# Attention and FFN kernel: row sums folded by a chain of accumulating transfers into one product

## The chip, the cores and the metric

The kernel runs on one core of a Trainium2 chip. A core has a tensor engine (PE; its weight loads are listed as PEld), a vector engine (DVE), a scalar engine (ACT), GpSimd (POOL), a sync engine (SP) that here only issues transfers, and sixteen DMA engines that all queues share. The metric is the device time of one execution in microseconds.

## The reference

The input x is (2, 2048, 512) in float32. One pre-norm transformer block is computed: layer norm, attention with 16 query heads and 2 key/value heads of 32 dimensions with rotary embedding, a residual, a second layer norm, a product with a weight that has been rounded to e4m3 (activations too), and a residual.

```python
scores = jnp.einsum('bqhd,bkhd->bhqk', q, k_exp) * hd ** (-0.5)
attn = jax.nn.softmax(scores, axis=-1)
out = jnp.einsum('bhqk,bkhd->bqhd', attn, v_exp).reshape(b, s, d)
return out @ wo + bo
...
x = x + _L0_attn_ref(_layernorm(x, axis=-1), ...)
x = x + _L0_ffn_ref(_layernorm(x, axis=-1), L0_ffn_weight)
```

What matters below is the softmax: each query's exponentials are summed over all 2048 keys, and the sum of exponentials times values is divided by that sum.

## The kernel before, in words

The tokens are cut into 8 blocks of 512, four per batch. Keys and values of the first batch are projected in a front part. Then the attention runs over 64 *units*: 8 blocks x 4 groups of four heads ("quads") x 2 halves of 256 queries. Side work (projections of the next block, the output product of the last one, second layer norms, the weight's rounding) is cut into small steps; `fill` puts one step at fixed places in the order of instructions. A last part does the FFN.

A unit has four *rounds* (r = 0 to 3), each over four chunks of 128 keys. The order is written out by hand (line 997 on). In a round PE computes:

- eight scores `s` (L517) for the *next* unit's row maxima, each into one of three PSUM banks, from which DVE takes a maximum (L524, into `part`). `more_scores(n)` emits n of them. When side work holds one of the three banks (`lent[0]` is not None), scores have two;
- four `T` (L963), the scores of this unit minus their maxima, 128 keys x (4 heads x 256 queries), alternating between two PSUM areas E and O. ACT makes `p = exp(T)` from each (L972), into four buffers in turn;
- the value products `avs` (L913) of the four p, 32 matmuls, into the first half of a PSUM bank `avs`.

The sums over keys are not made by PE from every p. POOL adds p of chunks 0 and 1 into `pair` (two buffers) and p of chunks 2 and 3 into a tile of `far_sums` (four buffers, L946 for both). Then a transfer that POOL issues adds `pair` to `far_sums[r]` in SBUF (`accum_op=add`, 512 KB, L1020). In round 2 one more such transfer adds `far_sums[0]` to `far_sums[1]` (L1022). So a unit leaves three tiles to be summed, 1 to 3 of `far_before` as the next unit calls them. That next unit multiplies them with ones on PE (`sum_up`, L927, eight matmuls for each tile) into the second half of its own `avs` bank: two tiles at the end of its round 0, the third at the end of its round 1. After that a job `finish_heads` copies the sums to `both[:, 1]` (L885), DVE takes two reciprocals (L889), and POOL multiplies values and reciprocals (L890). `both[:, 0]`, the values, is copied from `avs` at the unit's end (L1038); `both` has one buffer.

Every engine executes its queue in order. A POOL instruction that waits for a transfer holds all that POOL has behind it, and so does a PE matmul that waits for a tile.

Of the kernel before, what the change touches and what calls it, by code (L numbers as in the profile page):

```python
# [8 lines left out]
F32 = mybir.dt.float32  # L9
# [4 lines left out]
ALU = mybir.AluOpType  # L14
AX = mybir.AxisListType

P = 128
# [10 lines left out]
def preln_attn_fp8_ffn_kernel(  # L28
# [37 lines left out]
    nc = tc.nc  # L66
# [9 lines left out]
    HB = 256  # L76
# [16 lines left out]
    w2 = ctx.enter_context(tc.tile_pool(name="w2", bufs=6))  # L93
# [13 lines left out]
    lent = [S_BANKS - 1]  # L107

    def s_bank():

        if s_next[0] == lent[0]:
            s_next[0] = (s_next[0] + 1) % S_BANKS
        tag = f"s{s_next[0]}"
        s_next[0] = (s_next[0] + 1) % S_BANKS
        return tag
# [354 lines left out]
    units = [(k, half) for k in range(len(quads)) for half in range(HALVES)]  # L470
# [28 lines left out]
    def split_maxima():  # L499

        if split:
            mview, mx = split.pop()
            nc.gpsimd.tensor_tensor(
                mview[:, :, :, 1], mx, mview[:, :, :, 0].bitcast(F32), ALU.subtract
            )
# [131 lines left out]
    def fetch_y_over_keys(n, what, g):  # L637

        y_near[n] = stacked[what][:, g, :].bitcast(F32).rearrange("p (i d) -> p i d", i=NT)
        nc.sync.dma_start(y_near[n], y_far[n])  # L640
# [122 lines left out]
    def fill(kind, pieces=1):  # L763

        for _ in range(pieces):
            ready = [job for job in queue if job.due <= step[0] and not job.waits()]
            if lent[0] is not None:
                ready = [job for job in ready if job is owner[0]]
            able = [
                (jobs, job)  # L770
                for jobs, some in ((finishing, finishing[:1]), (queue, ready), (beside, beside))
                for job in some
                if job.kind in (kind, OTHER) and job.due <= step[0]
            ]
            if able:
                do(*able[0])
# [41 lines left out]
    def stack_next(u):  # L818
        k, half = units[u]
        n, quad = quads[k]  # L820

        if half == 0:
            if k + 1 < len(quads) and k + 1 not in qst:
                while quads[k + 1] not in q_raw:
                    advance()
                stack_queries(k + 1)
        b = batch(k)
        if b + 1 < B and n == (b + 1) * NB - 1 and quad == 2 and half == 1:
            while (b + 2) * NB - 1 not in keys_done:
                advance()  # L830
            fetch_keys("kS", b + 1, 0)
            fetch_keys("dkS", b + 1, 0)
        if b > 0 and n == b * NB and quad == 0 and half == 0:
            fetch_keys("kS", b, 1)
            fetch_keys("dkS", b, 1)
# [69 lines left out]
    def columns(u, chunks, probs, av):  # L905

        k, half = units[u]
        for kc, p in zip(chunks, probs):
# [3 lines left out]
            for j in range(4):  # L912
# [7 lines left out]
                    skip_group_check=True,  # L920
                )

    def sum_up(dst, parts, start, stop):

        for i, part in enumerate(parts):
            for j in range(4):
                nc.tensor.matmul(  # L927
                    dst[j * HD : (j + 1) * HD, :],
                    ones,
                    part[:, j, :],  # L930
                    start=start and i == 0,
                    stop=stop and i == len(parts) - 1,
                    tile_position=(0, j * HD),
                    skip_group_check=True,
                )

    def add_pair(u, kc, a, b):
        far = kc % ROUND == 2
        pa = papool.tile(
            [P, 4, HB],  # L940
            F32,
            tag="pa" if far else "pair",
            name=f"pa_{u}_{kc}",
            bufs=4 if far else 2,
        )
        nc.gpsimd.tensor_tensor(pa, a, b, ALU.add)  # L946
        return pa

    def probabilities(u, T, kc):

        k, half = units[u]
        if kc < 2:
            for j in range(4):
                nc.tensor.matmul(  # L954
                    T[:, j, :],
                    sel[:, j, :],
                    maxima[u],
                    start=(j % 2 == 0),
                    stop=True,
                    skip_group_check=True,  # L960
                )
        for j in range(0, 4, 2):
            nc.tensor.matmul(  # L963
                T[:, j : j + 2, :],
                stacked["dkS"][:, group(k), kc * P : (kc + 1) * P],
                qst[k][:, j : j + 2, half * HB : (half + 1) * HB],
                start=False,
                stop=True,
                skip_group_check=True,
            )  # L970
        p = ppool.tile([P, 4, HB], F32, tag="p", name=f"p_{u}_{kc}")
        nc.scalar.activation(p, T, AF.Exp, scale=SCALE)  # L972
        return p

    def more_scores(n):
        for _ in range(n):
            next(scores, None)

    with tc.manual_schedule():
        more_scores(LEAD)  # L980
        for u, (k, half) in enumerate(units):
            n, quad = quads[k]
            if half == 0 and quad == 0:
                attn_of[n] = wide.tile(
                    [P, QUADS, TB], F32, tag="attn", name=f"attn_{n}", bufs=2
                )
            stack_next(u)
            banks = [
                ps_t.tile([P, 4, HB], F32, tag="EO"[parity], name=f"T_{u}_{parity}")
                for parity in range(2)  # L990
            ]

            far_sums = []
            whole = u == len(units) - 1
            ending_soon = u >= len(units) - 2
            pieces = 2 if ending_soon else 1
            for r in range(ROUNDS):
                chunks = list(range(r * ROUND, (r + 1) * ROUND))
                step[0] += 1
                while r == 1 and landing:  # L1000
                    landing.pop()()
                if r == 2:
                    ask(u)
                last = r == ROUNDS - 1
                more_scores(2 if r == 0 else 1)
                probs = [probabilities(u, banks[0], chunks[0])]
                more_scores(0 if r == 0 else 1)
                probs.append(probabilities(u, banks[1], chunks[1]))
                pair = add_pair(u, chunks[0], *probs)
                more_scores(2)  # L1010
                if r > 0:
                    fill(ON_PE, pieces)
                probs.append(probabilities(u, banks[0], chunks[2]))
                more_scores(2)
                probs.append(probabilities(u, banks[1], chunks[3]))
                if ending_soon:
                    fill(ON_DVE)
                if not (last and whole):
                    far_sums.append(add_pair(u, chunks[2], *probs[2:]))
                    nc.gpsimd.dma_start(out=far_sums[r], in_=pair, accum_op=ALU.add)  # L1020
                if r == 2:
                    nc.gpsimd.dma_start(out=far_sums[1], in_=far_sums[0], accum_op=ALU.add)  # L1022
                fill(ON_PE, pieces)
                more_scores(2)
                split_maxima()
                fill(ON_DVE, 3 if finishing else 2)
                if r == 0:
                    avs = ps_av.tile([P, 2, HB], F32, tag="av", name=f"avs_{u}")
                columns(u, chunks, probs, avs[:, 0, :])


                if u > 0 and r == 0:
                    sum_up(avs[:, 1, :], far_before[1:3], False, False)
                elif u > 0 and r == 1:
                    sum_up(avs[:, 1, :], far_before[3:], False, True)
                    finishing.append(Job(finish_heads(u - 1, both, avs[:, 1, :])))
            both = w2.tile([P, 2, HB], F32, tag="both", name=f"both_{u}", bufs=1)
            nc.scalar.copy(both[:, 0, :], avs[:, 0, :])  # L1038
            far_before = far_sums
        sums = ps_s.tile([P, TB], F32, tag=s_bank(), name="sums_last")[:, :HB]  # L1040
        sum_up(sums, [pair, *probs[2:], *far_sums[1:]], True, True)
        finishing.append(Job(finish_heads(u, both, sums)))
        fetch_y_over_keys(2, "kS", 1)
        attending[0] = False
        for jobs in (finishing, queue, beside):
            while jobs:
                jobs[0].step()
                if jobs[0].kind is None:
                    jobs.pop(0)
# [122 lines left out]
```

## Time and profile before

| | |
|---|---|
| median of 3 runs | 2327.25 us (2326.39 to 2331.35) |
| profiled execution | 2329.9 us |
| span of its instructions | 2327.9 us |
| mean granted PE clock | 0.975 |
| PE busy | 2141.7 us (92%) |
| DVE busy | 1706.0 us (73%) |
| POOL busy | 1766.2 us (76%) |
| ACT busy | 1237.9 us (53%) |
| transfers by POOL's queue (q0) | 175.66 MB, 40.1% of sixteen engines' span |

A line of the profile names the source line, the engine, the operation, the tiles written and read, and how often. "[0.72 <-ACT p L972]" is the engine's idle time ahead of it and what ended it. In a table of windows, each engine has its busy time in that stretch and, in brackets, the number of its instructions; the last three columns are the granted PE clock as a share of full speed, the share of the sixteen DMA engines' time that was busy, and GB/s. The attention takes up about 126 to 2215 us of the span; the 64 units in it take 27.3 to 43.6 us each.

### The profile page before, as it was taken

The numbers are of one execution on the slowest core, as the hardware profiler recorded it, in microseconds if no ns is written. First come the engines' busy times: TensorE is split into PE (matmuls) and PEld (weight loads), VectorE is DVE, ScalarE is ACT, GpSimd is POOL, SyncE is SP. The second block draws the span as 40 slices with busy tenths as digits, with TensorE's granted clock in tenths as the row PEclk, the third lists the DMA queues.
The fourth block names the chain that finished last, engine by engine and source line by source line (L and its number), as shares of the span: only waits on it lengthen the run. The fifth ranks groups of instructions, "written<-read, shape, count | busy, mean of one in ns | idle before, by whom it ended". The sixth has DMA issues, their size and how long they took to land. (4 is left out here: it accounts for less than half of the span.)

```text
span 2327.9 us, 39404 instructions
## 1 busy us (share of the span) xinstructions
PE 2141.7 (92%) x15506; PEld 1239.0 (53%) x15506; DVE 1706.0 (73%) x2679; ACT 1237.9 (53%) x1545; POOL 1766.2 (76%) x1199
## 2 busy tenths in 40 slices
PE   5499999999999999999999999999999899899945
PEld 3255555555555555555555555555555555555522
DVE  3467778776777776876777778676977977767578
ACT  2146556655556555655555555554655555545546
POOL 3268889988877987889878878887888777877810
PEclk9699999999999999999999999999999999999978
DMA  6646656666466765658486556664665645847512
GB/s 197 169 102 137 136 114 163 143 141 131 94 163 135 158 129 135 145 121 194 99 206 141 108 124 147 133 118 95 135 149 120 141 99 126 171 89 196 109 55 109
DMA packets 116410, 312.76 MB, mean 134 GB/s; under 512 B 16896, under 2 KB 17536, under 8 KB 112384
## 3 DMA queue, kind: packets, MB, share of 16 engines
q0 software_dynamic: 50160, 175.66, 40.1%
q1 hardware_dynamic: 63648, 133.21, 19.4%
q8 instruction: 121, 1.98, 0.3%
q10 hardware_dynamic: 2416, 1.38, 0.2%
q14 instruction: 65, 0.53, 0.1%
HBM read 91.56 MB, written 42.99 MB: 58 GB/s over the span
## 5 line engine op out<-in xcount | busy, mean ns | idle before, releaser
L524 DVE TENSOR_REDUCE part<-s 128x1 f32<-128x512 f32 x2048 | 1312.8, 684 | 525.4 <-PE s L517 523.5
L946 POOL TENSOR_TENSOR pa<-p,p 128x1024 f32<-128x1024 f32 x511 | 1241.4, 2479 | 283.6 <-ACT p L972 261.2
L972 ACT ACTIVATE p<-T 128x1024 f32<-128x1024 f32 x1024 | 1002.5, 1024 | 583.0 <-PE T L963 554.6
L517 PE MATMUL s<-kS,qst 128*128 128x512 f32 x2048 | 865.9, 465 | 89.2 <-DVE part L524 27.2
L963 PE MATMUL T<-qst,dkS 128*128 128x512 f32 x2048 | 698.2, 423 | 3.1 <-ACT p L972 2.0
L517 PEld LDWEIGHTS s<-kS,qst 128*128 128x128 f32 x2048 | 383.3, 190 | 491.8 <-DVE part L524 277.8
L913 PE MATMUL avs<-p,vX 128*32 128x256 f32 x8192 | 509.5, 383 | 1.1 <-ACT p L972 1.1
L963 PEld LDWEIGHTS T<-qst,dkS 128*128 128x128 f32 x2048 | 366.3, 189 | 138.7 <-issue 52.0
L913 PEld LDWEIGHTS avs<-p,vX 128*32 128x32 f32 x8192 | 233.6, 110 | 214.3 <-issue 79.6
L1020 POOL DMA_DIRECT2D pa<-pa x255 | 224.2, 879 | 80.4 <-POOL pa L946 75.6
L301 PE MATMUL po<-wo_sb,attn 128*128 128x512 f32 x256 | 130.2, 594 | 1.3 <-POOL attn L890 1.3
L889 DVE RECIPROCAL both<-both 128x128 f32<-128x128 f32 x128 | 112.4, 919 | 11.2 <-ACT both L885 11.2
L301 PE MATMUL pq<-xnT_q,wq_sb 128*128 128x512 f32 x224 | 114.3, 592 | 0.0
L927 PE MATMUL avs<-pa,ones 128*32 128x256 f32 x1512 | 105.5, 382 | 6.8 <-DMA pa<-pa 6.8
L885 ACT COPY both<-avs 128x256 f32<-128x256 f32 x63 | 23.4, 372 | 133.2 <-PE avs L927 133.2
L890 POOL TENSOR_TENSOR attn<-both 128x256 f32<-128x256 f32 x64 | 84.8, 1326 | 5.9 <-DVE both L889 5.9
L954 PEld LDWEIGHTS T<-mT,sel 128*128 128x128 f32 x512 | 78.4, 189 | 13.0 <-ACT mT L546 1.5
L954 PE MATMUL T<-mT,sel 128*128 128x256 f32 x512 | 81.7, 282 | 0.6 <-ACT mT L546 0.6
L1022 POOL DMA_DIRECT2D pa<-pa x64 | 74.2, 1159 | 5.4 <-DMA pa<-pa 5.0
L927 PEld LDWEIGHTS avs<-pa,ones 128*32 128x32 f32 x1512 | 49.3, 111 | 39.8 <-DMA pa<-pa 7.3
L546 ACT CAST mT<-mtp 128x256 fp32r<-128x256 f32 x64 | 23.8, 371 | 84.1 <-PE mtp L542 84.1
L532 ACT CAST mrow<-mx 128x8 fp32r<-128x8 f32 x64 | 13.1, 205 | 93.6 <-DVE mx L531 93.6
(126 smaller groups left out, 1157.5 us busy)
## 6 DMA issues: line engine op xcount, KB each, us to landing
pa<-pa POOLq DMA_DIRECT2D x319, 512.0 KB, 4.9
qst<-q_far SPq DMA_DIRECT2D x128, 256.0 KB, 4.6
x_kv<-in_L_attn_x_dram SPq DMA_DIRECT2D x8, 1024.0 KB, 8.7
q_far<-hi_q SPq DMA_DIRECT2D x32, 256.0 KB, 4.4
q_far<-lo_q SPq DMA_DIRECT2D x32, 256.0 KB, 3.7
x_res<-in_L_attn_x_dram SPq DMA_DIRECT2D x8, 1024.0 KB, 8.8
x_res<-in_L_attn_bo_dram POOLq DMA_DIRECT2D x8, 1024.0 KB, 11.8
out_dram<-v SPq DMA_DIRECT2D x16, 512.0 KB, 2.8
```

Of the source, the lines that this page charges most:

```text
L301: nc.tensor.matmul(dst, lhs(c), rhs(c), start=(c == 0), stop=(c == chunks - 1))
L517: nc.tensor.matmul(s, qst[k][:, j, at : at + P], stacked["kS"][:, group(k), kb * TB : (kb + 1) * TB], start=True, stop=True,)
L524: nc.vector.tensor_reduce(part[:, i, j, kb : kb + 1], s, AX.X, ALU.max)
L889: nc.vector.reciprocal(piece, piece)
L890: nc.gpsimd.tensor_tensor(attn_of[n][:, quad, half * HB : (half + 1) * HB], both[:, 0, :], both[:, 1, :], ALU.mult)
L913: nc.tensor.matmul(av[j * HD : (j + 1) * HD, :], vX[batch(k)][:, kc, group(k), :], p[:, j, :], start=(kc == 0), stop=(kc == NTS - 1), tile ...
L927: nc.tensor.matmul(dst[j * HD : (j + 1) * HD, :], ones, part[:, j, :], start=start and i == 0, stop=stop and i == len(parts) - 1, tile_pos ...
L946: nc.gpsimd.tensor_tensor(pa, a, b, ALU.add)
L954: nc.tensor.matmul(T[:, j, :], sel[:, j, :], maxima[u], start=(j % 2 == 0), stop=True, skip_group_check=True,)
L963: nc.tensor.matmul(T[:, j : j + 2, :], stacked["dkS"][:, group(k), kc * P : (kc + 1) * P], qst[k][:, j : j + 2, half * HB : (half + 1) * H ...
L972: nc.scalar.activation(p, T, AF.Exp, scale=SCALE)
L1020: nc.gpsimd.dma_start(out=far_sums[r], in_=pair, accum_op=ALU.add)
```

## The change

For every unit but the last three (`in_one`), two more accumulating transfers are issued in the next unit: tile 1 is added to tile 2 after the first addition of round 0, and tile 2 to tile 3 after the first addition of round 1. Tile 3 then holds the whole unit's sums, and one `sum_up` of eight matmuls follows at the end of round 2 in place of those at the ends of rounds 0 and 1. The finishing starts a round later. `both` gets a second buffer. And where a bank is lent at the start of rounds 1 to 3, both scores ahead of the second probability are now emitted ahead of the first one, as round 0 always does.

```diff
+    def in_one(u):
+
+        return 0 <= u < len(units) - 3
+
...
                 last = r == ROUNDS - 1
-                more_scores(2 if r == 0 else 1)
+
+                before = 1 if r > 0 and lent[0] is None else 2
+                more_scores(before)
                 probs = [probabilities(u, banks[0], chunks[0])]
-                more_scores(0 if r == 0 else 1)
+                more_scores(2 - before)
                 probs.append(probabilities(u, banks[1], chunks[1]))
                 pair = add_pair(u, chunks[0], *probs)
+
+                if r < 2 and in_one(u - 1):
+                    at = r + 2
+                    nc.gpsimd.dma_start(
+                        out=far_before[at], in_=far_before[at - 1], accum_op=ALU.add
+                    )
                 more_scores(2)
...
-                if u > 0 and r == 0:
+                if u > 0 and r == 0 and not in_one(u - 1):
                     sum_up(avs[:, 1, :], far_before[1:3], False, False)
-                elif u > 0 and r == 1:
+                elif u > 0 and r == (2 if in_one(u - 1) else 1):
                     sum_up(avs[:, 1, :], far_before[3:], False, True)
                     finishing.append(Job(finish_heads(u - 1, both, avs[:, 1, :])))
-            both = w2.tile([P, 2, HB], F32, tag="both", name=f"both_{u}", bufs=1)
+            both = w2.tile([P, 2, HB], F32, tag="both", name=f"both_{u}", bufs=2)
             nc.scalar.copy(both[:, 0, :], avs[:, 0, :])
             far_before = far_sums
```

## The prediction

> **What bounds the kernel now.** I read the page first, then the waits, then the timeline of TensorE (PE) and of GpSimd (POOL) for single units, then windows cut at the first score-of-probability matmul (T<-qst,dkS) of each round.
>
> ```profile
> PE 2141.7 (92%) x15506; PEld 1239.0 (53%) x15506; DVE 1706.0 (73%) x2679; ACT 1237.9 (53%) x1545; POOL 1766.2 (76%) x1199
> ...
> q0 software_dynamic: 50160, 175.66, 40.1%
> ...
> L927 PE MATMUL avs<-pa,ones 128*32 128x256 f32 x1512 | 105.5, 382 | 6.8 <-DMA pa<-pa 6.8
> ```
>
> PE looks like the bound, and the products with ones (L927) hold 105.5 us of it. But three engines stand above 70%, so what a product is worth has to be read inside a round. The PE timeline of one unit, the ends of its rounds 0, 1 and 2:
>
> ```profile
> 1007.14 1.93 PE L913 MATMUL avs<-p,vX 128*32 128x256 f32 x32
> 1008.89 1.05 PE L927 MATMUL avs<-pa,ones 128*32 128x256 f32 x16
> 1009.87 0.50 PE L517 MATMUL s<-kS,qst 128*128 128x512 f32 x1
> ...
> 1015.71 1.93 PE L913 MATMUL avs<-p,vX 128*32 128x256 f32 x32
> 1017.46 0.61 PE L927 MATMUL avs<-pa,ones 128*32 128x256 f32 x8
> 1018.01 0.50 PE L517 MATMUL s<-kS,qst 128*128 128x512 f32 x1
> ...
> 1022.34 1.94 PE L913 MATMUL avs<-p,vX 128*32 128x256 f32 x32
> 1024.20 0.50 PE L517 MATMUL s<-kS,qst 128*128 128x512 f32 x1
> ```
>
> From the first value product to the next score it takes 2.73, 2.30 and 1.86 us: each eight sum matmuls cost 0.43 to 0.44 us, on PE's own path, since the score follows without a wait. POOL in an idle unit (so I call one without side work on PE; the others are full ones):
>
> ```profile
> 1678.78 4.73 POOL L946 TENSOR_TENSOR pa<-p,p 128x1024 f32<-128x1024 f32 x2 [0.72 <-ACT p L972]
> 1683.81 0.87 POOL L1020 DMA_DIRECT2D pa<-pa  x1 [0.30 <-POOL pa L946]
> 1684.39 1.18 POOL L1022 DMA_DIRECT2D pa<-pa  x1
> ```
>
> Two additions, a transfer's issue, and idle time of 0.72 us: POOL is close behind PE. A second issue directly after the first moves POOL's end from 1684.68 to 1685.57: 0.89 us each. Windows over whole units (span, PE, PEld, DVE, ACT, POOL, clock, DMA share, GB/s):
>
> ```profile
> 1032.40:1066.80 34.40, 33.77 (x243) 19.47 (x242) 23.18 (x38) 18.62 (x24) 33.13 (x22) 1.00 0.81 190
> 1600.30:1634.20 33.90, 33.17 (x240) 19.16 (x239) 24.48 (x40) 17.40 (x21) 24.22 (x16) 1.00 0.44 89
> ```
>
> In the first POOL's 33.13 us plus four waits of 0.30 us leave nothing; in the second 8.5 us are free. And the DMA engines in rounds 1 and 2 of a unit that begins a block, with the landing of the two pair transfers issued there:
>
> ```profile
> 1440.30:1446.90 6.60, 6.57 (x58) 3.98 (x57) 5.08 (x8) 4.08 (x5) 6.14 (x4) 1.00 0.77 188
> 1446.90:1453.10 6.20, 6.17 (x50) 3.76 (x49) 5.97 (x10) 4.23 (x6) 2.19 (x3) 1.00 1.04 300
> ```
>
> ```profile
> DMA to landing us min/median/max: 9.0/9.8/10.5
> ```
>
> There the engines are full; over the whole kernel the median landing is 4.7 us. POOL is busy for only 2.19 of 6.2 us there: it waits for a landing already.
>
> **The change, part by part.** The profiled execution took 2329.9 us (span 2327.9), 2.65 above the median of the runs, 2327.25; I sum against 2329.9 and take the difference to the median.
>
> *Sum matmuls.* For 61 units (u-1 from 0 to 60) 24 become 8: 16 fewer, 2 x 0.435 = 0.87 us, 61 x 0.87 = 53.1 us. The vector engine (DVE) would hide some if it were busy when the score is ready; before the first reduction of rounds 1 and 2 it sits idle 0.35 to 2.1 us in the units I read, so I count nothing back. The page's busy time would say 105.5 x 16/24 x 61/63 = 68; it holds the tails of matmuls that overlap.
>
> *POOL's two added issues.* 122 issues between the two additions of rounds 0 and 1, 0.89 us each: 1.8 us a unit. Taking each unit's POOL busy time plus 4 x 0.30 from its length, 49 of 61 units have over 2.67 us idle (0.87 + 1.8) and lose nothing. Twelve don't: those starting at 188.6, 354.1, 410.7, 767.6 and 1032.4 have about none (shortfall 2.59 to 2.66 each, 13.1 together), those at 501.8 and 1993.1 have 1.07 (1.6 each), five more fall short by 0.14 to 0.93 (2.4). Together 18.7 us given back. Inside an idle unit, rounds 0 and 1 need 2 x 2.35 + 0.89 + 1.16 = 6.75 us of POOL in a PE round of 6.2, and the buffer of p for the third chunk was free only 1.8 us ahead: about 0.45 us late in ten such units, 5 us (0 to 12).
>
> *The transfers' landing.* 122 more of 512 KB; q0 moves 175.66 MB in 40.1% of 2328 us, so one takes 2.79 us of all sixteen engines, 340 in all: the DMA share goes from 0.62 to about 0.78. The product of round 2 now waits for a chain of two. Behind it on PE's queue stands everything: scores, probabilities, value products. In a quiet unit the second link is issued after the first addition of round 1, lands 4.7 us later, and is needed 6.7 us or more after its issue: hidden. Where q0 is backed up I put its landing at the later of issue + 4.7 and the round-0 pair's landing + 2.8, against the end of round 2's value products less 1.31 us. Thirteen units come out late: those starting at 382.8, 1171.1, 1433.0, 1690.6 and 1965.2 by 5.0, 5.6, 6.0, 5.2 and 4.1 us, eight others by 0.2 to 2.4, 38.7 in all. Off this come 5.1 in three units that POOL holds anyhow, 2.5 that two of them wait already, and about 3 at 2029, where PE now waits 6.84 us for such a landing (POOL's buffers will hold it there still, but later). I take 28, with ends of 5 (a landing of 4.5, the shortest, hides most) and 60 (17.4, the longest that a chained transfer had).
>
> *PE's clock.* Behind that wait of 6.84 us the granted clock falls:
>
> ```profile
> 2021.60:2037.50 15.90, 8.74 (x69) 4.77 (x68) 4.62 (x9) 4.00 (x5) 10.06 (x10) 0.79 1.05 209
> 2037.50:2047.20 9.70, 9.70 (x61) 6.04 (x61) 5.25 (x8) 4.18 (x5) 5.76 (x5) 0.81 0.62 116
> ```
>
> Its next round takes 9.57 where its like takes 8.2: 1.4 us. Five units are late by over 4 us: 5 of at most 7 us. The Trainium skill speaks against the change here: its page "TensorE: Matmul & The Clock Gate", Part 1, says that the clock halves after an idle window of about 3.4 us and needs as long a busy one to return. By the page's window, the five longest waits would all drop the clock and the other eight would not, an estimate of the same five units.
>
> The page "DMA: Bandwidth & Descriptors", section on the anatomy of one DMA, gives about 2.0 us plus bytes over 436 GB/s, 3.2 us for 512 KB. No transfer of this kind landed in under 4.5 here; by the page's figure the lateness would shrink by about 1.3 us a unit, an estimate that I don't use.
>
> *First products by the lent bank.* With a bank lent, rounds 1 to 3 issue both scores before the first probability. Reductions that follow without waiting start 0.60 us apart, the second one now 0.69: the fourth score, which waits for it, comes 0.1 to 0.14 us earlier in some 80 rounds, 8 to 11 us; against it the first exponential and POOL's first addition start 0.23 us later. I take -6 (-11 to +6).
>
> *Finishing a round later.* Two reciprocals of 0.92 us move from the end of round 2 to that of round 3; round 3's third score waits 0.62 us for DVE in an idle unit, 0.13 in a full one. I take -4 (-16 to 0). The copy of the values at a unit's end would now meet the POOL product of the finishing still reading its buffer; the second buffer takes that wait away and costs nothing, and without it the copy, next unit's value bank and PE would wait. POOL's product (L890) moves past one round of POOL's queue and waits for reciprocals there, before the next unit's first exponentials: nothing. SP's queue is not touched, but its loads share the engines, which is in the lateness above.
>
> Sum: -53.1 + 18.7 + 5 + 28 + 5 - 6 - 4 = -6.4. 2329.9 becomes 2323.5, the median about 2321.
>
> **Rivals.** *PE waits for the chain (slower).* One mechanism: sums at round 2 of units that begin a block, behind loads that fill the DMA engines. It decides once the lateness kept exceeds 39 us instead of 28 (3 us a unit over thirteen), which backed-up queues can well give, as each added transfer also delays the pairs behind it: at 60 us and 7 for the clock, +27, 2354. The full DMA rounds speak for it, the quiet units (0.44) against. *POOL becomes the bound, the gain is eaten:* shortfalls of 25 instead of 23.7 and no gain from the two reorderings: about +5 against the -6.4, within 0.2%: 2327. *The loads turn out hidden:* lateness of 5, clock 0: -34, 2293. *The product moves without getting fewer or the finishing shifts side work into other units:* the counts above exclude the first, and side work has idle units to go to; small.
>
> **How the numbers follow.** 0.2% of 2327 (4.65 us) is about what can be told from no change. Forecast, the saving survives in part (to 2322.6 and down to 2305): 0.30. Loads hidden (below 2305): 0.17. Eaten, within 0.2%: 0.15. PE waits for the chain: 0.38. So faster 0.47, same 0.15, slower 0.38. The range takes the bounds together: low 2288 (lateness near nothing), high 2350 (lateness near 55). The likeliest case alone spans 2305 to 2323.
>
> **What would show it.** Right: 24 sum matmuls a unit become 8, all in round 2; quiet units shorter by about 0.9 us; POOL in the idle units over 95% busy; PE's waits on "DMA pa<-pa" at the sum's line in the units that begin a block, with clock dips. Wrong: no such wait (then it is faster than said), idle units longer than before (POOL), or landings of 512 KB over 6 us in quiet units, too.

## The result, and the profile after

The changed kernel takes 2369.64 us (median of 4 runs, 2363.57 to 2371.49) beside 2328.82 us for the kernel before on the same chip: a ratio of 1.0173, 95% interval [1.0159, 1.0187], or 40 us (37 to 44) more. The forecast was 2321 us, 6 us less, and its range ended at 2350. Its span is 2367.8 us and its mean granted clock 0.958 (before 0.975). In the changed file the sums are L931 (L927 before), POOL's additions L950 (L946), the two added transfers L1018 (called links below), the pair transfer L1031 (L1020) and the exponentials L976 (L972).

The page, the rows for POOL's queue, the sum products and the landing of all accumulating transfers (the last figure is the median in us):

```profile
q0 software_dynamic: 67728, 239.63, 53.9%
...
L931 PE MATMUL avs<-pa,ones 128*32 128x256 f32 x536 | 44.4, 408 | 31.9 <-DMA pa<-pa 31.9
...
pa<-pa POOLq DMA_DIRECT2D x441, 512.0 KB, 5.4
```

The products fell from 1512 to 536 as meant. POOL's queue grew by 64 MB, the median landing of all accumulating transfers from 4.9 to 5.4 us. In a quiet unit TensorE (PE) does what was forecast. Its timeline in the unit shown before (start, duration), the ends of rounds 0 and 2:

```profile
1027.74 1.93 PE L913 MATMUL avs<-p,vX 128*32 128x256 f32 x32
1029.60 0.73 PE L517 MATMUL s<-kS,qst 128*128 128x512 f32 x2
...
1041.54 1.93 PE L913 MATMUL avs<-p,vX 128*32 128x256 f32 x32
1043.29 0.61 PE L931 MATMUL avs<-pa,ones 128*32 128x256 f32 x8
1043.84 0.50 PE L517 MATMUL s<-kS,qst 128*128 128x512 f32 x1
```

The sixteen sum matmuls that stood after round 0's value products are gone, and eight stand after round 2's. This unit takes 29.24 us instead of 30.63. The loss is in others. The waits of the whole kernel (us in total, times, longest):

```profile
ACT p L976 <- POOL pa L950: 89.6, 43, 8.5
...
PEld avs L931 <- DMA pa<-pa: 36.9, 11, 6.5
POOL pa L1018 <- DMA pa<-pa: 36.0, 15, 5.6
POOL pa L950 <- DMA pa<-pa: 35.0, 19, 5.4
```

The first is ACT waiting for a buffer of p that POOL has not yet added up. The others are a sum product, a link and an addition that wait for a transfer. The first wait in the kernel before:

```profile
ACT p L972 <- POOL pa L946: 21.6, 16, 4.6
```

The worst places are rounds 2. Of the eight that became longer by 5.0 to 9.3 us, five belong to units that begin a block, as the slower rival said. The other three belong to full units in the middle of a block, in which POOL had at most 1.1 us to spare before; there the second link waits 3.1 to 4.7 us for the first, and holds up POOL behind it. One of the five, the unit whose rounds 1 and 2 were shown before: its rounds 2 and 3 now as windows, and then from its timelines three lines of POOL and one of PE:

```profile
1477.15:1490.25 13.10, 7.91 (x58) 3.91 (x57) 5.34 (x9) 4.35 (x6) 9.49 (x6) 0.89 1.06 273
1490.25:1499.20 8.95, 8.95 (x57) 6.00 (x56) 7.31 (x11) 4.80 (x6) 7.68 (x7) 0.78 0.88 216
```

```profile
1478.59 0.87 POOL L1018 DMA_DIRECT2D pa<-pa  x1
...
1484.68 2.33 POOL L950 TENSOR_TENSOR pa<-p,p 128x1024 f32<-128x1024 f32 x1 [1.62 <-DMA pa<-pa]
1488.70 2.36 POOL L950 TENSOR_TENSOR pa<-p,p 128x1024 f32<-128x1024 f32 x1 [1.69 <-DMA pa<-pa]
```

```profile
1488.61 1.08 PE L931 MATMUL avs<-pa,ones 128*32 128x256 f32 x8 [4.05 <-DMA pa<-pa]
```

The second link, due in round 1, is issued in round 2, at 1478.59, with the DMA engines full (a share of 1.06). PE's product, which needs it, waits 4.05 us and starts at 1488.61, two additions wait for transfers that still hold their buffers, and round 2 takes 13.10 us instead of 6.20. The next round runs at a granted clock of 0.78. The page "TensorE: Matmul & The Clock Gate" of the Trainium skill, Part 1, gives about 3.4 us of idling after which the clock halves; this wait and the round behind it agree with that.

Summed over all units but the last, round 0 became 41 us shorter, round 1 8, round 3 22, and round 2 111 us longer.

### The profile page after: what moved, and what is told of

It is laid out like the page before. It is cut to its first block, busy times and chain, and to the rows that moved or that the text cites. A ratio compares the mean times of both kernels' runs of the same rounds, so it can differ in the third digit from the quotient of the medians.

```text
span 2367.8 us, 37574 instructions
## 1 busy us (share of the span) xinstructions
PE 2117.6 (89%) x14525; PEld 1220.9 (52%) x14530; DVE 1723.8 (73%) x2679; ACT 1238.4 (52%) x1545; POOL 1876.3 (79%) x1321
## 3 DMA queue, kind: packets, MB, share of 16 engines
q1 hardware_dynamic: 63648, 133.21, 18.9%
## 4 chain that ended last, share of the span: by engine, by line
PE 48%; POOL 15%; DVE 14%; DMA 12%; ACT 4%; issue 3%; SPq 0%; DVEq 0%; POOLq 0%; ACTq 0%
PE s L517 14%; PE T L967 11%; PE avs L913 11%; POOL pa L950 10%; DMA pa<-pa 9%; DVE part L524 6%; PE po L301 4%; ACT p L976 3%; PE pq L301 3%; DVE sw_q L319 2%; PE T L958 2%; PE avs L931 1%; DVE both L889 1%; POOL pa L1018 1%; POOL pa L1031 1%
## 5 line engine op out<-in xcount | busy, mean ns | idle before, releaser
L950 POOL TENSOR_TENSOR pa<-p,p 128x1024 f32<-128x1024 f32 x511 | 1285.2, 2561 | 176.6 <-ACT p L976 136.3
L976 ACT ACTIVATE p<-T 128x1024 f32<-128x1024 f32 x1024 | 1002.3, 1024 | 653.2 <-PE T L967 550.5
L517 PE MATMUL s<-kS,qst 128*128 128x512 f32 x2048 | 845.7, 467 | 106.7 <-DVE part L524 43.2
L967 PE MATMUL T<-qst,dkS 128*128 128x512 f32 x2048 | 690.5, 428 | 16.4 <-ACT p L976 15.5
L913 PE MATMUL avs<-p,vX 128*32 128x256 f32 x8192 | 522.7, 388 | 8.2 <-ACT p L976 8.0
L967 PEld LDWEIGHTS T<-qst,dkS 128*128 128x128 f32 x2048 | 372.5, 193 | 163.2 <-issue 56.3
L1031 POOL DMA_DIRECT2D pa<-pa x255 | 223.5, 876 | 82.8 <-POOL pa L950 78.5
L1018 POOL DMA_DIRECT2D pa<-pa x122 | 111.3, 912 | 36.3 <-DMA pa<-pa 36.0
L889 DVE RECIPROCAL both<-both 128x128 f32<-128x128 f32 x128 | 112.5, 920 | 12.6 <-ACT both L885 12.6
L1033 POOL DMA_DIRECT2D pa<-pa x64 | 73.8, 1153 | 5.0 <-PE s L517 5.0
L931 PE MATMUL avs<-pa,ones 128*32 128x256 f32 x536 | 44.4, 408 | 31.9 <-DMA pa<-pa 31.9
L890 POOL TENSOR_TENSOR attn<-both 128x256 f32<-128x256 f32 x64 | 66.6, 1041 | 7.4 <-DVE both L889 7.4
L319 DVE SCALAR_TENSOR_TENSOR sw_q<-sw_q,sign,cs 128x512 f32<-128x512 f32 x30 | 66.0, 2200 | 0.4 <-DMA sw_q<-q 0.2
```

What stands on the lines that cost most here:

```text
L319: nc.vector.scalar_tensor_tensor(t[:rows], t[:rows], sign[:rows], csb[:rows, 1, :], ALU.mult, ALU.mult)
L517: nc.tensor.matmul(s, qst[k][:, j, at : at + P], stacked["kS"][:, group(k), kb * TB : (kb + 1) * TB], start=True, stop=True,)
L889: nc.vector.reciprocal(piece, piece)
L913: nc.tensor.matmul(av[j * HD : (j + 1) * HD, :], vX[batch(k)][:, kc, group(k), :], p[:, j, :], start=(kc == 0), stop=(kc == NTS - 1), tile ...
L967: nc.tensor.matmul(T[:, j : j + 2, :], stacked["dkS"][:, group(k), kc * P : (kc + 1) * P], qst[k][:, j : j + 2, half * HB : (half + 1) * H ...
L1018: nc.gpsimd.dma_start(out=far_before[at], in_=far_before[at - 1], accum_op=ALU.add)
```

## The experiments

Every difference below is a ratio to the kernel before, run on the same chip, times 2327.25 us. A term measured as the difference of two such ratios is uncertain by some 5 us. The runs go from the kernel before to the change one part at a time, so the parts add up to the whole by construction. What a part is worth could differ in another order. Some of the kernels leave out sums or read a constant tile in place of a sum, as their expectations say, and serve for timing alone.

**The parts that were to gain.** First the order of scores alone, on the kernel before:

```diff
-                more_scores(2 if r == 0 else 1)
+                before = 1 if r > 0 and lent[0] is None else 2
+                more_scores(before)
                 probs = [probabilities(u, banks[0], chunks[0])]
-                more_scores(0 if r == 0 else 1)
+                more_scores(2 - before)
```

> The kernel before with nothing but the new order of the first scores where a bank is lent. My estimate was -6 us (-11 to +6), a ratio of 0.997; theory O says slower, 1.003 or more, since the first exponential comes 0.23 us later.

Measured: 0.9964 [0.9952, 0.9977], -8.4 us. Then also two buffers and the finishing in round 2, with the sums still in rounds 0 and 1 and no links; against the changed kernel:

```diff
...
-                if u > 0 and r == 0 and not in_one(u - 1):
+                if u > 0 and r == 0:
                     sum_up(avs[:, 1, :], far_before[1:3], False, False)
-                elif u > 0 and r == (2 if in_one(u - 1) else 1):
+                elif u > 0 and r == 1:
                     sum_up(avs[:, 1, :], far_before[3:], False, True)
+                if u > 0 and r == (2 if in_one(u - 1) else 1):
                     finishing.append(Job(finish_heads(u - 1, both, avs[:, 1, :])))
```

> New order of first scores, two buffers for the values and the finishing queued in round 2 instead of 1; the sums stay in rounds 0 and 1 as before, and there are no added transfers. As forecast: order -6 to -8 and finishing later -4: 2315 (2308 to 2319). Rival: the -56.5 of the kernel without added transfers is 7.8 of order and 48.7 of matmuls, 53.1 were forecast for these, so finishing later costs 0 to 4: 2319 to 2324.

Measured: 2307.44 us, 0.9910 [0.9895, 0.9925], so -12.6 us for the finishing. DVE's timelines at the start of the same unit's round 3, which begins at 758.37 us with the order alone (first fence) and at 757.47 us with late finishing (second):

```profile
757.62 1.75 DVE L889 RECIPROCAL both<-both 128x128 f32<-128x128 f32 x2
759.28 4.80 DVE L524 TENSOR_REDUCE part<-s 128x1 f32<-128x512 f32 x8
```

```profile
757.67 5.09 DVE L524 TENSOR_REDUCE part<-s 128x1 f32<-128x512 f32 x8 [0.28 <-PE s L517]
762.68 1.75 DVE L889 RECIPROCAL both<-both 128x128 f32<-128x128 f32 x2
```

The reductions now start 0.20 us after the round instead of 0.91, and the round takes 7.39 us, not 7.84.

Last the whole change without its links:

```diff
-                if r < 2 and in_one(u - 1):
-                    at = r + 2
-                    nc.gpsimd.dma_start(
-                        out=far_before[at], in_=far_before[at - 1], accum_op=ALU.add
-                    )
```

> The changed kernel without its two chain transfers; the product still takes only the third tile, so two thirds of each unit's sums are left out. It keeps the 16 fewer sum matmuls, the later finishing, the second buffer and the order of the first scores. Theory L (the links' landings, behind loads that fill the DMA engines, hold POOL and PE; the rest of the change pays): -53 for the matmuls, -6 for the order, -4 for the later finishing, so about 2266 (ratio about 0.973). Theory O (the later finishing or the new order of the scores costs): 2300 or more.

Measured: 2270.62 us, 0.9754 [0.9740, 0.9767], -57.2 us in all. So the matmuls gave only -36.3 us against the kernel with late finishing. By units, from the two traces: 15 are shorter by the full 0.87 us each, nine by more (16 us together), 30 by about 0.5, and the other nine come out 7 us longer together. One of the 30 shows why. DVE, with the matmuls gone (first fence) and with them (second), at the start of its round 1, where a step of side work (L319) precedes the reduction:

```profile
860.70 1.78 DVE L319 SCALAR_TENSOR_TENSOR sw_q<-sw_q,sign,cs 128x512 f32<-128x512 f32 x1
862.40 2.56 DVE L524 TENSOR_REDUCE part<-s 128x1 f32<-128x512 f32 x4
```

```profile
876.97 2.68 DVE L524 TENSOR_REDUCE part<-s 128x1 f32<-128x512 f32 x4 [0.39 <-PE s L517]
```

With the matmuls the reduction waited 0.39 us for PE's score; without them DVE is still at L319 when the score is ready. Round 1 there got shorter by 0.07 us, not by 0.43. Ten more of the 30 go the same way: 0.3 to 0.4 us of idle time on DVE ahead of that reduction, gone without the matmuls. In 14 others the loss is in round 2, which becomes 0.6 to 0.85 us longer, where the eight sum matmuls that it now holds account for 0.43. In one of these, side work on POOL (L335, L336) sets when that round's additions start; in another, side work on ACT (L260, L263) stands ahead of its exponentials. For the rest the cause stays open.

**POOL's two issues.** The links were cut to 16 numbers of each partition, 8 KB:

```diff
-                        out=far_before[at], in_=far_before[at - 1], accum_op=ALU.add
+                        out=far_before[at][:, 0, :16],
+                        in_=far_before[at - 1][:, 0, :16],
+                        accum_op=ALU.add,
```

> The changed kernel with both links cut to 16 numbers of each partition (8 KB instead of 512 KB): every instruction, issue and wait of the change is there, the bytes are not; nearly all of two tiles is left out of the sums. Theory P (POOL's 0.89 us for each of 122 issues makes it the bound): it keeps most of the loss, 2340 or more. Theory L: POOL's issues give back 24 of the 63 us of the kernel without links, about 2290 (ratio about 0.983), and PE's waits on pa at the sum are gone.

Measured: 2323.37 us, 0.9978 [0.9969, 0.9988], 52 us above the kernel without links. The same small links behind the pair transfer, at the ends of rounds 0 and 1, where POOL seemed to have time:

> As the small links (16 numbers of each partition, nearly all of two tiles left out of the sums), but issued after the pair's transfer at the end of rounds 0 and 1, not between the round's two additions. The small links cost 52.8 us over no links, 0.43 us for each issue, where I had counted 24. Theory P1 (place: between the additions POOL has no idle time, the second addition and the exponentials behind it wait; ahead of a round's first addition POOL idles 1.1 us): under 2295. Theory P2 (POOL's time as such): stays at 2315 to 2330.

Measured: 2444.44 us, 1.0495 [1.0470, 1.0519]. That was a surprise of 120 us. POOL's timeline at the worst place:

```profile
411.64 1.19 POOL L1028 DMA_DIRECT2D pa<-pa  x1
412.20 3.05 POOL L950 TENSOR_TENSOR pa<-p,p 128x1024 f32<-128x1024 f32 x1
424.06 2.34 POOL L950 TENSOR_TENSOR pa<-p,p 128x1024 f32<-128x1024 f32 x1 [8.81 <-DMA pa<-pa]
```

The second addition writes into the buffer from which the link (L1028) still reads; it waits 8.81 us for it. The kernel's waits of additions for transfers (in all, times, longest), 150.8 us of them for these links:

```profile
POOL pa L950 <- DMA pa<-pa: 157.7, 74, 8.8
```

A link does not only wait: it holds the buffer of a sum that the next unit's addition needs. To take this away the small transfers read a constant tile instead:

```diff
-                        in_=far_before[at - 1][:, 0, :16],
+                        in_=wq_sb[:, 0, :16],
```

> Two added issues of 8 KB in each unit, at the ends of rounds 0 and 1 right behind the pair transfer, and from a constant tile instead of the earlier sum, so that no buffer of sums has to wait for them; the sums of tiles 0 to 2 are left out. Theory P (an issue between the two additions of a round makes the second addition late, at the end of the round it lies in idle time): most of the 52.8 us of the small transfers between the additions is gone: 2271 to 2290, and a wait of PE for the second small transfer of up to 25 us on top. Rival: each issue costs its 0.43 us wherever it stands: 2323 or more. Against the small transfers at the same place but from the earlier sum (2444): theory S (there the second addition waited for its buffer, which the small transfer was still reading, up to 8.8 us) expects the 121 us between them gone.

Measured: 2339.00 us, 1.0044 [1.0027, 1.0061]: 105 us of the 120 are gone, and the additions' waits for transfers fall to 17.1 us. POOL had no wait of a link for the other one in either kernel, and PE's waits at L931 are close to each other (62.8 and 54.1 us), so the buffer was the reason. But PE waited here, too, for the second small transfer, and that hid what the place itself is worth:

```profile
PE avs L931 <- DMA pa<-wq_sb: 54.1, 24, 7.3
```

So the small transfers went into a spare tile that nothing reads, at the ends of rounds 0 and 1, and between the additions as the change has them:

```diff
...
+                        out=spare[r], in_=wq_sb[:, 0, r * 16 : r * 16 + 16], accum_op=ALU.add
```

> Two added issues of 8 KB in each unit, from a constant tile into a spare one that nothing reads, at the ends of rounds 0 and 1 behind the pair transfer; the sums of tiles 0 to 2 are left out. Nothing waits for them. Theory P (an issue costs where it makes the second addition of a round late; at the end it lies in POOL's idle time): 2271 to 2285. Theory R (an issue takes its 0.43 us on average wherever it stands): about 2320.

> The same two issues between the additions of rounds 0 and 1; the sums of tiles 0 to 2 are left out. Theory P: the small transfers between the additions took 2323, of which 8 and 3 us were waits of POOL and TensorE for such a transfer: 2308 to 2316. Theory W (most of the 52 us were waits for landings): 2271 to 2295.

Measured: 0.9880 [0.9861, 0.9898] at the ends (2299.61 us), 0.9965 [0.9948, 0.9982] between the additions (2320.12 us). Against 0.9754 without links, two issues on POOL cost 49 us between the additions and 29 at the ends, with nothing waiting for a transfer of theirs. Neither theory got it: the place is worth 20 us, the bare issue 29. The waits of ACT for POOL over the whole kernel, without links, with the issues in between, with them at the ends:

```profile
ACT p L976 <- POOL pa L950: 30.5, 17, 7.8
ACT p L982 <- POOL pa L956: 73.2, 50, 6.0
ACT p L982 <- POOL pa L956: 74.3, 56, 7.2
```

The additions' waits for transfers, the other way in which the small transfers could have cost time, did not grow (27.9, 22.2 and 19.6 us). Between the additions the loss lies in rounds 1 and 2 (15 and 27 us in all; rounds 0 and 3 have 4 and 1). Where it goes, in the timeline of POOL in one idle unit: without links, with the issues in between, with them at the ends (round 2 starts at 932.01, 959.08 and 945.54):

```profile
928.41 4.72 POOL L950 TENSOR_TENSOR pa<-p,p 128x1024 f32<-128x1024 f32 x2 [0.49 <-ACT p L976]
...
935.73 4.73 POOL L950 TENSOR_TENSOR pa<-p,p 128x1024 f32<-128x1024 f32 x2
```

```profile
957.92 1.15 POOL L1023 DMA_DIRECT2D spare<-wq_sb  x1
...
964.08 4.73 POOL L956 TENSOR_TENSOR pa<-p,p 128x1024 f32<-128x1024 f32 x2
```

```profile
947.93 1.16 POOL L1034 DMA_DIRECT2D spare<-wq_sb  x1
...
950.51 4.72 POOL L956 TENSOR_TENSOR pa<-p,p 128x1024 f32<-128x1024 f32 x2
```

Without links POOL has 0.49 us to spare ahead of round 1's additions; then three small steps of a layer norm (L206 to L208, 1.7 us) stand at the head of round 2, and its additions follow without a gap, 3.72 us after the round's start. With either pair of issues they start 5.00 or 4.97 us after it, and round 2 takes 7.45 or 7.42 us instead of 6.81. POOL has idle time in this unit, but not in these two rounds. Between the additions 36 units lose over 0.3 us, 55.7 us in all; the 20 units that take under 30 us without links have 18.9 of the net 46 us.

**The bytes and the chain.** Two full transfers at the links' places, from a constant tile and into tiles that neither the other transfer nor the product waits for:

```diff
-                        out=far_before[at], in_=far_before[at - 1], accum_op=ALU.add
+                        out=far_before[at - 1], in_=fixed, accum_op=ALU.add
```

> The two added transfers keep their place and their 512 KB, but go from a constant tile into the first and second sum, so that neither the second one waits for the first nor the product for either; the sums of tiles 0 to 2 are left out. Theory C (the 46 us between small and full transfers are the two waits for landings): about 2341, as the separate removals of the two waits gave 15 and 13 us; 2323 if the waits are all of it. Theory B (the bytes themselves: other loads land later, buffers come free later): 2355 to 2370, with POOL or PE waiting for DMA elsewhere.

Measured: 2348.51 us, 1.0085 [1.0070, 1.0100]. Between the two theories: 28 us above the spare transfers of 8 KB at the same place are the price of the bytes, together with the buffers that transfers into sums hold; the 20.5 us up to the change are the price of the chain. A wait of this kernel that the spare transfers don't have:

```profile
POOL pa L952 <- DMA pa<-wq_sb: 33.9, 20, 5.3
```

That is again an addition that waits until a link lets its buffer go. The landing of the queries' loads (256 KB, from SP's queue; the last figure is the median) in those two kernels:

```profile
qst<-q_far SPq DMA_DIRECT2D x128, 256.0 KB, 4.5
qst<-q_far SPq DMA_DIRECT2D x128, 256.0 KB, 6.2
```

How the 28 us divide between the buffers and the later loads is open.

Other pairings take one wait of the chain away each. In the first, shown here, both links add into tile 2, so that PE waits for none; in the second, ((1, 2), (3, 2)), tile 2 is added into 1 and into 3, so that the second link does not wait for the first; in the third, ((1, 3), (2, 3)), tile 3 is added into 1 and 2:

```diff
-                    at = r + 2
+                    to, of = ((2, 1), (2, 3))[r]
...
-                        out=far_before[at], in_=far_before[at - 1], accum_op=ALU.add
+                        out=far_before[to], in_=far_before[of], accum_op=ALU.add
```

> The changed kernel with full links in their places between other tiles (2 += 1, then 2 += 3): POOL waits as in the change, but PE's product reads tile 3 alone, which no link writes; two tiles are left out of the sums. If PE's own wait for the chain (36.9 us of idle time before the sum's weight loads in the changed kernel) is on the path: about 2335. If POOL's waits hold the same rounds anyway: 2360 or more.

> The changed kernel with full links between other tiles (1 += 2, then 3 += 2): the second link does not wait for the first, PE's product waits for the second as in the change; one tile is left out of the sums. If POOL's wait at the second link (35 us in the changed kernel) is on the path: about 2345. If not: 2365 or more.

> The changed kernel with both links at full size and in place, but between other tiles (1 += 3, then 2 += 3), so that no link waits for the other and the product, which reads tile 3 alone, waits for none; two thirds of the sums are left out. Theory L in its narrow form (the two waits in order are the loss): about 2300, within 15 us of the small links. Theory D (the traffic itself is the loss: pair transfers, query loads and buffers come late whoever waits for the links): 2345 or more.

Measured: 1.0116 [1.0095, 1.0137], 1.0125 [1.0108, 1.0142] and 1.0218 [1.0193, 1.0242]. Each wait is worth 11 to 13 us. The third came out slower than the change: its first link waits for the pair transfer issued just ahead of it (41.3 us of POOL's waits, all 18 for that transfer). So it does not show both waits taken away together; the constant tile does. Issuing the links earlier, the first at the end of the unit itself and the second at the end of the next round 0, brought nothing:

```diff
...
+                if r == 3 and in_one(u):
+                    nc.gpsimd.dma_start(out=far_sums[2], in_=far_sums[1], accum_op=ALU.add)
+                if r == 0 and in_one(u - 1):
+                    nc.gpsimd.dma_start(
+                        out=far_before[3], in_=far_before[2], accum_op=ALU.add
+                    )
```

> A full kernel: the same two links, but each a round earlier and at a round's end behind the pair's transfer: 2 += 1 at the end of the unit's own round 3, 3 += 2 at the end of the next unit's round 0; one product at the end of round 2 as in the change. Theory P1 with landings that now have one to two rounds of time: 2285 to 2305, faster than both. Theory D (the traffic of 122 more transfers costs wherever it is): 2340 or more.

Measured: 1.0164 [1.0149, 1.0179]. Against the change, round 1 is 27 us longer in all, rounds 0, 2 and 3 are 32 us shorter.

**Versions.** The links only in 24 units that are quiet, chosen from the traces, with the sums elsewhere as before:

```diff
...
     def in_one(u):
 
-        return 0 <= u < len(units) - 3
+        return u + 1 in QUIET
```

> The chain of transfers and the single product are kept in 24 units alone (those that were shorter than in the kernel with the new order of scores by 0.5 us or more in the profile after); the other units take their sums in rounds 0 and 1 as before. Theory L (the costs are local: an addition on POOL that comes late and a landing that comes late, in crowded units): the 24 units keep their gains, 33 us together by the two traces, on top of the 2319 of the new order alone: 2286 (2278 to 2300). Theory T (the costs travel: more bytes on the same engines, lower clock for all): the mean loss per unit of the change against the new order alone is 50/61 = 0.8 us, so 24 units cost 20: 2339.

Measured: 2299.12 us, 0.9873 [0.9851, 0.9894]. The losses are mostly local: 23 of the 24 chosen units are shorter than with the order alone, and the 24 save 30 us; the others lengthen by 8 together, which the theory of local costs did not have. And with late finishing in all units and the links in 22:

> New order of first scores, two buffers, finishing in round 2 in all units, and the chain with its single product in 22 units alone, those that got shorter against the kernel that finishes late without a chain, or that the run with 24 such units showed to be quiet. If the parts add up: 2307.4 - 17 clean units x 0.86 = 2293 (2288 to 2298). Rival: finishing later and the chain share one gain, since both move DVE's reciprocals out of a round: 2299 as for the 24 units with early finishing elsewhere, or more.

Measured: 2299.03 us, 0.9868 [0.9847, 0.9889]. The parts don't add up. Against the kernel with late finishing alone 12 of the 22 units save 0.8 us or more, four about half of that and one loses. The other five save nothing here (they lose 0.1 to 0.2 us), but save 0.8 to 0.9 us each, against the same kernel, in the version with 24 units, where the units ahead of them finish early: the two gains are in part one, as the rival said. Two units that begin a block, without links, lose 2.8 and 3.1 us; why stays open. Both versions beat the kernel before by 1.3%.

## Why the prediction was wrong

The same sum with the measured terms (ratios above):

| term | forecast, us | measured, us |
|---|---|---|
| sum matmuls | -53.1 | -36 |
| POOL's two added issues | +23.7 | +49 |
| landing and clock | +33 | +48 (chain 20.5, bytes and held buffers 28) |
| first products by the lent bank | -6 | -8 |
| finishing a round later | -4 | -13 |
| sum | -6.4 | +40 |

*Sum matmuls.* The 0.87 us of a unit is right and stands in each quiet unit. The step that failed is "so I count nothing back": the cover on DVE was looked for in a few units, and 30 others keep only about half of the 0.87. The prediction's own reading had the bound in it: where DVE sat idle for only 0.35 us ahead of the reduction, taking 0.87 us of matmuls away could give back little more. Four units that had 0.34 or 0.35 us there kept 0.5 us each.

*POOL's two added issues.* This is the largest miss, 25 us. The price of one issue, 0.89 us, was right. The step that failed set each unit's idle time on POOL against 2.67 us, as if idle time in round 3 could serve an issue in round 1. The additions of a round are due in that round, because ACT needs the buffers of p (its waits for them rise from 30.5 to 73.2 us with the issues alone). In the unit shown, side work on POOL stands in a clump at a round's head. And the rounds that the matmuls, the order and the finishing shorten leave POOL less room than the lengths of before: its idle time ahead of additions that wait for ACT was 261.2 us before and is 189.7 without links. Instead of twelve units short and ten a little late by 0.45 us, 36 lost time. The rival "POOL becomes the bound" was the right mechanism, priced at 25 instead of 49; its own sum, +5, also makes 2332 us and not the 2327 that stands there.

*Landing and clock.* The mechanism that the prediction priced, the waits for the chain, was right: the profile shows eleven waits of PE, 36.9 us together, and the five units that were to be late by 5.0, 5.6, 6.0, 5.2 and 4.1 us wait 6.5, 6.5, 4.5, 3.8 and 3.5. In time the chain cost 20.5 us, less than the 33 that stood for it and the clock. The step that failed is what it put at nothing: full transfers cost another 28 us with nothing waiting for the chain. One part of that was left out: the links also hold the buffers of the sums, 16.2 of the 35.0 us for which POOL's additions wait after, and 33.9 us with the constant tile. I priced what waits for a link to land, not what waits for a buffer that it reads or writes to come free. Part of the 48 us is the clock: from 130 us to the end of the attention the granted clock stood at half for 20.5 us before, 51.2 with the spare transfers between the additions, 61.4 with the constant tile and 99.0 after. No run here separates that part; as PE loses at most half of such time, it is at most 24 us of the 48, an estimate from these figures.

*Order and finishing* had the right sign and lay within their ends, except that -13 was near the far one.

The slower rival had the sign, but not for its reason alone. By its own account, lateness, it would have ended near 2354, and with 15 us more for landing and clock than forecast and nothing else wrong the sum is +9: most of the loss came from terms that it held fixed. Its condition was a lateness of over 39 us; the chain alone did not cost that. For the same reason the range was too short above: only the lateness was moved to its bad end, while POOL's late additions ended at 12 us and the matmuls had no bound against them.

Of the signs named in the prediction, the fewer matmuls, shorter quiet units, waits at the sum's line and clock dips all came. POOL was to be over 95% busy in the idle units; of the fourteen units with links that took under 30 us before, only two reach 96%, so POOL's share of a unit does not show its loss. "Idle units longer than before" was named as the sign of POOL, and it came in ten of the fourteen, though some of these wait for links as well: the unit shown in POOL's timelines takes 29.09 us after and 28.70 before.

## What to carry to other kernels

An engine's free time counts only ahead of the instruction that is due: cut the windows at the deadlines, round by round, and take the lengths that the change itself will leave. For an added asynchronous transfer, price three things apart: its issue on the issuing engine's queue, what waits for it to land, and which buffer it keeps from its next writer. A saving read in a few units holds in units like those; it is worth asking whether the change can be made there and left out elsewhere.

## What the runs showed of the hardware

Two issues of 8 KB in each unit, 122 in all, cost 29 to 49 us here, and their landing depends on what was issued ahead of them. The spare transfers between the additions (first line) and right behind a pair transfer of 512 KB (second), issue to landing:

```profile
DMA to landing us min/median/max: 2.0/2.8/11.7
```

```profile
DMA to landing us min/median/max: 3.8/5.0/12.7
```

No sum was read or written there and nothing waited for them, so the 2.2 us between the medians go with the place; whether the queue or the busy DMA engines make them is not shown. On POOL such an issue took 0.87 us in the median between additions and 1.18 directly behind another issue, as much as one of 512 KB (0.87 and 1.18 in the kernel before). The page "DMA: Bandwidth & Descriptors" of the Trainium skill, section on the anatomy of one DMA, gives a fixed part of about 2.0 us; the shortest landing of 8 KB agrees with it. For 512 KB its formula gives 3.2 us, an estimate, and none of the accumulating transfers in the profiles before and after landed in under 4.5.
